# Layer 1's output, router and shared expert in blocks of 16 steps beside the recurrence

## The chip, the cores and the metric

The kernel runs on one core of a Trainium2 chip. The engines are PE (TensorE, matrix products; PEld is its weight load), DVE (VectorE), ACT (ScalarE), POOL (GpSimd) and SP (SyncE, which here only issues DMAs). The metric is the time of one execution in device microseconds; lower is better. The time before is the median of three runs.

## The reference, cut to what matters

The network has four layers on x (16 sequences of 128 steps, 256 features); each layer adds a mixing part and a feed-forward part to x. The change lies in layer 1. Its mixing part is a recurrence over the 128 steps, its feed-forward part a mixture of 64 experts, of which each token takes eight, and a shared expert:

```
def step(carry, xs):                      # 128 steps, all 16 sequences at once
    r, state = carry
    r = decay * r + kt * vt
    inp = (qt * r) @ Wi.T + bi
    gate = sigmoid(inp @ Wg.T + bg)
    blended = gate * state + (1 - gate) * inp
    state = tanh(blended @ A.T + inp @ Bm.T)
    out = state @ Wo.T + bo               # added to x

h = layernorm(x)                          # 2048 tokens of 256
logits = h @ router_w.T                   # 64 experts
topk_w, topk_ids = top_k(softmax(logits), 8)
topk_w = topk_w / sum(topk_w)
# each expert takes its first 128 tokens, in the order of the tokens
routed = segment_sum(expert(h[token]) * topk_w)
shared = silu(h @ ws_gate) * (h @ ws_up) @ ws_down
x = x + routed + shared
```

Only `gate * state`, the product with A and the tanh depend on the step before. Everything else of the recurrence is known ahead of it.

## The kernel before, in words

x stays in SBUF as 16 blocks of 128 rows by 256: block b is sequence b, a row is a step. A scheduler orders each engine's instructions from the order in which the program writes them and from what they depend on; it may pull an instruction ahead. `issue_after(i)` keeps what is written in it behind instruction i on i's engine.

**Layer 0** ends in `l0_rest`. It also makes, with `l1_pre`, what the recurrence needs of each step: `gate` and `pre`. Both have the layout (step, half of the features, sequence).

**The recurrence** is `l1_steps`. For each step PE adds `pre` (product with the identity) and `gate` times A (the products `ps_all<-wA,gate`) into a PSUM bank, one of three; ACT makes the tanh `th` (L964); DVE turns it into `state` (L966); DVE multiplies the next step's gate by it (L969); PE goes on with that. Beside it runs `side_work`: it makes ahead what layers 2 and 3 need of the context (keys, values, gates, head means, quantised weights). Its parts are closures with an engine, a cost and a gap, and `spread` gives each a step: a chain's parts follow each other, and the costs of one engine in one step stay under its `room`. In step s the parts are issued behind the last product, the tanh and the gate of that step.

**Behind the recurrence** come, for each sequence, the bias `bo` (L189, which nothing keeps behind the recurrence, so it stands where layer 0 ends), the output product of its 128 states with Wo, and the addition to x (L186). `l1_ffn` then takes four sequences at a time: norm (L161 to L170, the power on POOL at L152), a store of h to `rows` in DRAM, transpositions (L182), the router's products, the eight largest logits of each token (L1031) and the mask of the chosen (L1032, L1033). `l1_keys` turns the mask around, expert by token, and multiplies it by a falling count of the tokens (L1238). `l1_slots` takes the 128 largest keys of each expert in 16 rounds of MAX8 and 15 of MATCH_REPLACE (L1269, L1271) and turns them into `slot_tok`, a table of token numbers (L1287). Beside this run the weights of the chosen experts and the shared expert (`l1_widen`, `l1_narrow`), which is added to x; x is then stored to the first of three sums in DRAM.

**The experts**, `l1_experts`: for each of 32 pairs, POOL gathers the rows of both experts with `slot_tok` (L1102), PE transposes and multiplies, and POOL scatters the results with addition into the sums (L1159). Weights come over SP into a ring of 10 slots and 2 more (L1096 to L1100), four pairs ahead in the program. `l1_clear` fills the sums with zeros first (L1076). `l1_sum` loads x and the other two sums back (L1400, L1402) for layers 2 and 3, `l2_l3`.

Of the kernel before, what the change touches and what calls it, by code (L numbers as in the profile page):

```python
# [19 lines left out]
P = 128  # L20
# [10 lines left out]
RING, MORE = 10, 2  # L31
# [28 lines left out]
class Kernel:  # L60
    def __init__(self, ctx, tc, ins, out):
# [14 lines left out]
        self.wscale = self.pers.tile([P, 3], F32, name="wscale")  # L76
        self.ring = False

# [25 lines left out]
    def mm(self, out, lhsT, rhs, start=True, stop=True):  # L104
        return self.nc.tensor.matmul(out, lhsT, rhs, start=start, stop=stop)  # L105
# [49 lines left out]
    def norm_x(self, g):  # L155

        nc = self.nc
        st = self.small.tile([P, GB, 6], F32, tag="st", name="st")
        mv = self.small.tile([P, GB, 2], F32, tag="mv", name="mv")
        for i in range(GB):  # L160
            nc.vector.bn_stats(st[:, i], self.x[:, g * GB + i])  # L161
            nc.vector.bn_aggr(mv[:, i], st[:, i])
        r = self.rstd(mv[:, :, 1], GB)

        def end():
            less = self.small.tile([P, GB], F32, tag="less", name="less")
            nc.vector.scalar_tensor_tensor(less, mv[:, :, 0], -1.0, r, ALU.mult, ALU.mult)
            h = self.hpool.tile([P, GB, D], F32, tag="h", name="h")
            for i in range(GB):
                nc.scalar.activation(  # L170
                    h[:, i], self.x[:, g * GB + i], AF.Identity, bias=less[:, i:i + 1], scale=r[:, i:i + 1]
                )
            return h

        return end

    def transpose4(self, h, dst, g):

        for c in range(2):
            pt = self.psum("tp")  # L180
            for i in range(GB):
                self.nc.tensor.transpose(pt[:, i * P:(i + 1) * P], h[:, i, c * P:(c + 1) * P], self.ident)  # L182
            self.evac(dst[:, c, g * GT:(g + 1) * GT], pt)

# [10 lines left out]
    def front(self):  # L195
        right = self.right
        with ExitStack() as base:
# [12 lines left out]
            self.wpool = self.open(self.mids, "wring", RING)  # L210
            pool = self.open(right, "state", side="right")
            with ExitStack() as ctx:
                self.l1_steps(pool, rec, self.side_work(self.open(ctx, "side", 2)))
# [15 lines left out]
    def side_work(self, pool):  # L229
        nc, ins = self.nc, self.ins  # L230

        def load(**args):

            self.side_dma = nc.sync.dma_start(**args)

        self.pool = pool
        bank = {n: self.psum("mm") for n in ("turn", "keys", "gates", "ones")}
# [19 lines left out]
        def pair(p):  # L257
# [3 lines left out]
            def begin():  # L261
                s["c"] = self.ctx_pair(p)
                s["st"] = self.small.tile([P, 2, 6], F32, tag="st", name="st")
                s["mv"] = self.small.tile([P, 2, 2], F32, tag="mv", name="mv")
# [8 lines left out]

            def scale(i):
                if not i:
                    s["h"] = pool.tile([P, 2, D], F32, tag="h", name="h")
                nc.vector.tensor_scalar(
                    s["h"][:, i], s["c"][:, i], s["mv"][:, i, 0:1], s["r"][:, i:i + 1], ALU.subtract, ALU.mult
                )

            def turn():
                for c in range(2):
                    for i in range(2):
                        at = (c * 2 + i) * P
                        nc.tensor.transpose(bank["turn"][:, at:at + P], s["h"][:, i, c * P:(c + 1) * P], self.ident)

            def affine(c):
                if not c:
                    s["ct"] = pool.tile([P, 2, 2 * P], F32, tag="ct", name="ct")
                nc.scalar.activation(  # L290
                    s["ct"][:, c], bank["turn"][:, c * 2 * P:(c + 1) * 2 * P], AF.Identity,
# [3 lines left out]
            def keys(c):  # L295
                self.mm(bank["keys"][:, :2 * P], wk[:, c], s["ct"][:, c], c == 0, c == 1)

            def values():
                for bb in range(2):
                    at = 2 * P + bb * 64  # L300
                    for c in range(2):
                        self.mm(
                            bank["keys"][:, at:at + 64], s["ct"][:, c, bb * P:(bb + 1) * P], wv[:, c], c == 0, c == 1
                        )

            def keep():
                kvt = pool.tile([P, 3 * P], F32, tag="kvt", name="kvt")
                nc.scalar.copy(kvt, bank["keys"][:, :3 * P])
# [10 lines left out]
            def less():  # L319
                va = pool.tile([P, 2, 4, 65], F32, tag="va", name="va", bufs=2)  # L320
                nc.gpsimd.memset(va[:, :, :, 64:65], 1.0)
                nc.vector.tensor_tensor(
# [7 lines left out]
                ("DVE", 0.2, lambda: spread(0), 0), ("DVE", 0.4, lambda: spread(1), 2),  # L330
                ("DVE", 0.45, lambda: scale(0), 0), ("DVE", 0.45, lambda: scale(1), 0), ("PE", 0.45, turn, 0),
                ("ACT", 0.6, lambda: affine(0), 0), ("ACT", 0.6, lambda: affine(1), 0),
                ("PE", 0.43, lambda: keys(0), 0), ("PE", 0.43, lambda: keys(1), 0), ("PE", 0.45, values, 0),
                ("ACT", 0.5, keep, 0), ("DVE", 0.7, mean, 0), ("DVE", 0.2, share, 0), ("DVE", 0.7, less, 0),
            ]

        def group(g):
# [7 lines left out]
            def part(n, k):  # L345
                for b in range(GB):
                    self.mm(
                        bank["gates"][b * 32:b * 32 + 32, n * P:(n + 1) * P], wgate[:, k, n],
                        s["c"][:, k, b * P:(b + 1) * P], k == 0, k == 1,
                    )  # L350

            def keep():
                gc = pool.tile([P, 2 * P], F32, tag="gc", name="gc", bufs=1)
                nc.scalar.copy(gc, bank["gates"][:, :2 * P])
                load(out=self.gc_d[g], in_=gc)

            return [("SP", 0, begin, 3)] + [
                ("PE", 0.6, lambda n=n, k=k: part(n, k), 0) for n in range(2) for k in range(2)
            ] + [("ACT", 0.4, keep, 0)]

        def quantised(n, name):
# [5 lines left out]
            def begin():  # L367
                s["w"] = self.slot()[:, :2048]
# [7 lines left out]
            def total(i):  # L376
                nc.vector.tensor_reduce(
                    s["sums"][:, i:i + 1], quarter(i), AX.X, ALU.add, apply_absolute_value=True
                )

            def all_rows():
                for i in range(4):
                    self.mm(bank["ones"][:, :1], ones, s["sums"][:, i:i + 1], i == 0, i == 3)

            def scales():
                nc.vector.tensor_scalar(scale, bank["ones"][:, :1], 1.0 / (D * 1024), 1e-5, ALU.mult, ALU.max)
# [14 lines left out]
            return [("SP", 0, begin, 9)] + [("DVE", 0.65, lambda i=i: total(i), 0) for i in range(4)] + [  # L401
# [9 lines left out]
        for p in range(NB // 2):  # L411
            chains.append((1 + 13 * p, pair(p)))
            if p % 2:
                chains.append((13 * p - 5, group(p // 2)))
            if p % 2 == 0 and p < 6:
                chains.append((2 + 13 * p, quantised(p // 2, f"L2_ffn_w_{('gate', 'up', 'down')[p // 2]}T")))
        return self.spread(chains)

    def spread(self, chains):


        room = {"PE": 0.9, "ACT": 0.9, "DVE": 0.75, "SP": 1.0}
        used, out = {}, {}
        for at, parts in chains:
            last = None
            for engine, cost, f, gap in parts:
                if engine == "PE" and last in ("ACT", "DVE"):
                    at += 1
                last = engine
                while used.get((at, engine), 0.0) + cost > room[engine]:  # L430
                    at += 1
                used[at, engine] = used.get((at, engine), 0.0) + cost
                out.setdefault(at, []).append(f)
                at += 1 + gap
        return out
# [418 lines left out]


# [84 lines left out]
    def l1_steps(self, pool, rec, beside):  # L940
# [4 lines left out]
        wa, wo, gate, pre = w["A"], w["Wo"], w["gate"], w["pre"]  # L945
        state = pool.tile([P, 2, (P + 1) * NB], F32, name="state", bufs=1)
        sums = [self.psum("mm") for _ in range(3)]
        for ps in sums:
            nc.vector.memset(ps[:, :64], 0.0)
        for s in range(P):  # L950
            ps = sums[s % 3]
# [20 lines left out]
            if s in beside:  # L972

                with ExitStack() as order:
                    for i in (last, tanh, gated):
                        order.enter_context(self.tc.issue_after(i.ins))
                    for f in beside.pop(s):
                        f()
        for s in sorted(beside):
            for f in beside[s]:  # L980
                f()
        for b in range(NB):
            self.bias_to_x(b, w["bo"])

        def out(b):
            po = self.psum("mm")
            for c in range(2):
                self.mm(po[:, :D], state[:, c, b:P * NB:NB], wo[:, c], c == 0, c == 1)
            self.add_to_x(b, po[:, :D])

        self.l1_out = out


    def l1_ffn(self):
# [3 lines left out]
        nc, ins = self.nc, self.ins  # L998
        with self.tc.issue_after(self.side_dma.ins):
            rw, wsgu, wsd = self.weights(  # L1000
                "L1_ffn_router_wT", "L1_ffn_ws_gate_up", ins["L1_ffn_ws_down"].rearrange("(c p) n -> p c n", p=F1)
            )
        rows, sums = self.rows, self.expert_sums
        with self.tc.tile_pool(name="l1s", bufs=1, reuse_waits="tile") as keep:
            with self.tc.tile_pool(name="l1f", bufs=2, reuse_waits="tile") as pool:
                self.hpool = pool
                self.ht = pool.tile([P, 2, NTOK], F32, name="ht", bufs=1)
                lg = pool.tile([P, NB, NE], F32, name="lg", bufs=1)


                val = keep.tile([P, NB, TOPK], F32, name="val", bufs=1)
                pairs = pool.tile([P, NB // 2, 2, NE], F32, name="pairs", bufs=1)
# [1052 lines left out]
```

## Time and profile before

| | us |
|---|---|
| median of 3 runs (lowest, highest) | 1722.08 (1721.45, 1724.77) |
| the profiled execution | 1721.37 |
| its span | 1719.6 |
| layer 0, to 614 | 614 |
| recurrence, first tanh 614.14, last 800.25 | 187 |
| output, norm, router, 801 to 838.6 | 37.6 |
| search to first gather, 838.6 to 884 | 45.4 |
| experts, 884 to 1097 | 213 |
| layers 2 and 3, from 1097 | 623 |

The times of single instructions come from the profiled execution. A line of a timeline has the start and the duration in us, engine, line, operation, the tile that is written `<-` the tiles that are read, the shapes, a count, and in brackets how long the engine stood idle before it and what ended that. A line of a tile's view has the smallest, median and largest duration in ns and the starts of the first and the last. PEclk is the clock that was granted to PE, as a share of the full one.

### The profile page before, as it was taken

How to read it: one execution, taken by the hardware profiler on the slowest of the kernel's cores; microseconds unless marked ns; L12 is line 12 of the kernel's file. 1: busy time of each engine (PE TensorE's matmuls, PEld its weight loads, DVE VectorE, ACT ScalarE, POOL GpSimd, SP SyncE). 2: the span in 40 equal slices, each digit the busy share in tenths (PEclk: the TensorE clock that was granted, in tenths of full speed). 3: DMA queues.
4: the chain of work that ended last, by engine and by line, in shares of the span. 5: the costliest groups of instructions: out<-in, count | busy, mean ns of one | idle time of the engine just before them, and what ended most of it. 6: DMA issues, size and time to landing. Idle time of an engine off the chain costs nothing.

```text
span 1719.6 us, 29806 instructions
## 1 busy us (share of the span) xinstructions
PE 1540.7 (90%) x11567; PEld 1078.4 (63%) x11567; DVE 924.0 (54%) x2374; ACT 720.7 (42%) x2096; POOL 431.1 (25%) x423
## 2 busy tenths in 40 slices
PE   7999999998999887787889888348999999999998
PEld 5777776765444444445558666136777777777776
DVE  4565464557475545545852222267676665755641
ACT  1443343344343222222312222035556756766655
POOL 2001000002232300000447888411321321412211
PEclk9999999999999977867989999668999999999999
DMA  8000000100000211114699995860000100100000
GB/s 252 7 7 7 7 7 1 50 13 23 0 1 2 77 41 64 64 51 176 198 289 288 294 248 94 193 205 18 21 29 21 24 24 27 30 11 9 7 7 13
DMA packets 93053, 124.67 MB, mean 72 GB/s; under 512 B 19760, under 2 KB 73072, under 8 KB 92784
## 3 DMA queue, kind: packets, MB, share of 16 engines
q1 hardware_dynamic: 73072, 97.69, 17.9%
q0 software_dynamic: 12288, 18.88, 5.7%
q10 hardware_dynamic: 7552, 6.20, 1.1%
q8 instruction: 91, 1.49, 0.3%
q14 instruction: 50, 0.41, 0.1%
HBM read 94.68 MB, written 28.05 MB: 71 GB/s over the span
## 4 chain that ended last, share of the span: by engine, by line
PE 62%; DVE 15%; issue 8%; DMA 7%; POOL 4%; ACT 4%; SPq 0%; ACTq 0%; POOLq 0%; DVEq 0%
PE ps_all L105 40%; PE ps_mm L105 12%; DMA xg<-rows,slot_tok 3%; PE ps_av L105 2%; DMA sum<-y,slot_tok 2%; PE ps_sc L105 2%; POOL rstd L152 1%; DVE state L966 1%; PE ps_all L1818 1%; ACT th L964 1%; PE ps_tp L456 1%; DVE gate L969 1%; DMA w<-in_moe_down 1%; PE ps_all L1432 1%; DVE st L1410 1%
## 5 line engine op out<-in xcount | busy, mean ns | idle before, releaser
L152 POOL TENSOR_TENSOR rstd<-ve,nhalf 128x2 f32<-128x2 f32 (+2 forms) x77 | 58.0, 756 | 634.1 <-DVE ve L150 548.7
L1810 POOL TENSOR_TENSOR e<-e,rs 128x512 f32<-128x512 f32 x64 | 66.1, 1040 | 282.2 <-DVE rs L1809 266.5
L445 ACT ACTIVATE e<-ps_sc,nmax 128x128 f32<-128x128 f32 x256 | 89.9, 377 | 108.1 <-DVE nmax L441 108.1
L1159 POOL DMA_INDIRECT sum<-y,slot_tok x64 | 102.0, 1594 | 28.2 <-issue 13.1
L1807 ACT ACTIVATE e<-e,nmax 128x128 f32<-128x128 f32 x256 | 99.3, 391 | 11.7 <-DVE nmax L1798 11.3
L105 PE MATMUL ps_all<-xt,w 128*64 128x128 f32 (+1 forms) x1024 | 101.9, 286 | 1.6 <-issue 0.9
L105 PEld LDWEIGHTS ps_all<-xt,w 128*64 128x64 f32 (+1 forms) x1024 | 90.1, 169 | 16.4 <-issue 11.7
L964 ACT ACTIVATE th<-ps_all 128x64 f32<-128x64 f32 x128 | 28.6, 223 | 139.3 <-PE ps_all L105 138.2
L105 PE MATMUL ps_all<-wA,gate 128*16 128x64 f32 x2032 | 67.5, 268 | 14.4 <-DVE gate L969 9.1
L966 DVE STREAM_TRANSPOSE state<-th 128x64 f32<-128x64 f32 x128 | 31.4, 245 | 88.7 <-ACT th L964 88.7
L1432 PE MATMUL ps_all<-ident,h 128*128 128x128 f32 x168 | 29.1, 300 | 50.6 <-DVE h L1415 38.9
L105 PE MATMUL ps_all<-ident,pre 128*16 128x64 f32 x1024 | 46.8, 264 | 28.7 <-ACT th L964 27.6
L105 PE MATMUL ps_mm<-ht,wq 128*128 128x256 f32 x256 | 69.8, 396 | 0.7 <-ACT ht L113 0.7
L1102 POOL DMA_INDIRECT xg<-rows,slot_tok x64 | 63.6, 993 | 25.5 <-issue 9.7
L186 DVE TENSOR_TENSOR x<-x,ps_all 128x256 f32<-128x256 f32 x48 | 20.0, 416 | 93.0 <-PE ps_all L105 92.9
L105 PE MATMUL ps_mm<-ctxt,wk 128*128 128x256 f32 x256 | 66.8, 384 | 0.0
L105 PE MATMUL ps_mm<-wu,mt 128*128 128x256 f32 x256 | 66.0, 391 | 0.0
L105 PEld LDWEIGHTS ps_all<-wA,gate 128*16 128x16 f32 x2032 | 40.3, 115 | 38.7 <-DVE gate L969 38.3
L1415 DVE TENSOR_SCALAR h<-x,mv,rstd 128x256 f32<-128x256 f32 x112 | 46.2, 441 | 30.6 <-POOL rstd L152 29.9
L105 PE MATMUL ps_all<-ht,w3q 128*128 128x256 f32 x256 | 61.5, 389 | 0.7 <-ACT ht L1761 0.7
L1432 PEld LDWEIGHTS ps_all<-ident,h 128*128 128x128 f32 x168 | 19.8, 148 | 66.5 <-DVE h L1415 32.2
L105 PE MATMUL ps_all<-ht,w3v 128*128 128x256 f32 x256 | 60.9, 381 | 0.0
(364 smaller groups left out, 3706.4 us busy)
## 6 DMA issues: line engine op xcount, KB each, us to landing
w<-in_moe_gate_up SPq DMA_DIRECT2D x64, 384.0 KB
w<-in_moe_down SPq DMA_DIRECT2D x64, 96.0 KB
c_in<-in_ctx SPq DMA_DIRECT2D x16, 256.0 KB
sum<-w SPq DMA_DIRECT2D x8, 512.0 KB
w<-in_moe_down SPq DMA_DIRECT2D x64, 64.0 KB
ysum<-sum SPq DMA_DIRECT2D x16, 256.0 KB
low<-tops SPq DMA_DIRECT2D x12, 256.0 KB
va_d<-va SPq DMA_DIRECT2D x8, 260.0 KB
```

What stands on the lines that cost most here:

```text
L105: return self.nc.tensor.matmul(out, lhsT, rhs, start=start, stop=stop)
L152: nc.gpsimd.tensor_tensor(r, ve, self.nhalf[:, :n], ALU.pow)
L186: self.nc.vector.tensor_tensor(self.x[:, b], self.x[:, b], ps, ALU.add)
L445: nc.scalar.activation(e[:, i], src[:, i], AF.Exp, bias=nmax[:, i:i + 1], accum_out=ssum[:, i:i + 1])
L964: tanh = nc.scalar.activation(th, ps[:, :64], AF.Tanh)
L966: nc.vector.transpose(state[:, :, at:at + 32], th.rearrange("p (c n) -> p c n", c=2))
L1102: nc.gpsimd.indirect_dma_start(out=x, out_offset=None, in_=rows, in_offset=bass.IndirectOffsetOnAxis(ap=slot_tok[:, e:e + 1], axis=0),)
L1159: nc.gpsimd.indirect_dma_start(out=sums[e % len(sums)], out_offset=bass.IndirectOffsetOnAxis(ap=slot_tok[:, e:e + 1], axis=0), in_=y, in_o ...
L1415: nc.vector.tensor_scalar(h[:, i], src[:, i], mv[:, i, 0:1], r[:, i:i + 1], ALU.subtract, ALU.mult)
L1432: self.nc.tensor.transpose(pt[:, at:at + P], h[:, i, c * P:(c + 1) * P], self.ident)
L1807: nc.scalar.activation(e[:, i], e[:, i], AF.Exp, bias=nmax[:, i:i + 1], accum_out=ssum[:, i:i + 1])
L1810: nc.gpsimd.tensor_tensor(e, e, rs.unsqueeze(2).to_broadcast([P, 4, P]), ALU.mult)
```

## The change

x is turned to another order before the recurrence, so that a block of 128 rows is 16 steps of 8 sequences instead of 128 steps of one. Once 16 steps of the recurrence are done, everything of layer 1 that these 256 tokens need can be made: output product, bias, norm, router, best eight, keys, and for blocks 0 to 5 the shared expert. These are parts for `spread` like those of `side_work`. Block 7 and the shared expert of blocks 6 and 7 come behind the last step.

- `l0_rest`: x is stored to DRAM in the order (half of the sequences, step, sequence) and loaded back as 16 tiles of 128 tokens, on SP. Block q has the tiles q and q + 8.
- `l1_steps`: two PSUM banks for the sums instead of three, six for the beside work. Each block gives an urgent chain, from step 16q + 17, and a later one. PE's instructions in the parts keep the order in which they are written.
- `spread`: more room (ACT 1.15 for 0.9, DVE 0.95 for 0.75, POOL 1.4 is new), and stretches between "+T" and "-T" hold a PSUM bank alone.
- `side_work`: the scaling of h and the absolute sums of the weights go from DVE to ACT, the difference of the head means from DVE to POOL; the key products are one part; chains start every 10 steps instead of 13. The quantised weights use a buffer of the side pool instead of the ring.
- The silu of the shared expert is made of a tanh in the blocks.
- The ring of the expert weights is opened after the side pool is closed. Three slots that held the router's tables, logits and keys join it behind `l1_slots` (15 slots for 12).
- `l1_slots` turns token numbers into the new row order; `l1_sum` reads the sums in that order.

```diff
 # front
-            self.wpool = self.open(self.mids, "wring", RING)
+            self.keep = self.open(self.mids, "tables", OLD)
             pool = self.open(right, "state", side="right")
             with ExitStack() as ctx:
-                self.l1_steps(pool, rec, self.side_work(self.open(ctx, "side", 2)))
+                self.l1_steps(pool, rec, self.open(ctx, "side", 2))
+            self.wpool = self.open(self.mids, "wring", RING)
             with self.tc.issue_after(self.side_dma.ins):
                 self.l1_clear()
 # side_work
-                nc.vector.tensor_scalar(
-                    s["h"][:, i], s["c"][:, i], s["mv"][:, i, 0:1], s["r"][:, i:i + 1], ALU.subtract, ALU.mult
+                nc.scalar.activation(
+                    s["h"][:, i], s["c"][:, i], AF.Identity, bias=s["less"][:, i:i + 1], scale=s["r"][:, i:i + 1]
                 )
...
-                nc.vector.tensor_tensor(
+                nc.gpsimd.tensor_tensor(
                     va[:, :, :, :64].rearrange("p b h d -> p (b h) d"), s["heads"],
...
-                ("PE", 0.43, lambda: keys(0), 0), ("PE", 0.43, lambda: keys(1), 0), ("PE", 0.45, values, 0),
+                ("PE", 0.86, keys, 0, "+K"), ("PE", 0.45, values, 0), ("ACT", 0.5, keep, 0, "-K"),
+                ("DVE", 0.7, mean, 0), ("DVE", 0.2, share, 0), ("POOL", 1.4, less, 0),
...
-            return [("SP", 0, begin, 9)] + [("DVE", 0.65, lambda i=i: total(i), 0) for i in range(4)] + [
+            return [("SP", 0, begin, 9)] + [("ACT", 0.65, lambda i=i: total(i), 0) for i in range(4)] + [
                 ("PE", 0.4, all_rows, 0), ("DVE", 0.4, scales, 0)
 # spread
-        room = {"PE": 0.9, "ACT": 0.9, "DVE": 0.75, "SP": 1.0}
+        room = {"PE": 0.9, "ACT": 1.15, "DVE": 0.95, "POOL": 1.4, "SP": 1.0}
 # l0_rest
+        by_half = x_t.rearrange("(h s b) d -> h s b d", h=2, s=P)
+        for g in range(NG):
+            at = g % 2 * GB
+            nc.sync.dma_start(out=by_half[g // 2, :, at:at + GB], in_=self.x[:, g * GB:(g + 1) * GB])
+        by_tile = x_t.rearrange("(t p) d -> p t d", p=P)
+        for at in range(0, 8, 2):
+            for half in range(2):
+                ts = slice(half * 8 + at, half * 8 + at + 2)
+                nc.sync.dma_start(out=self.x[:, ts], in_=by_tile[:, ts])
 # l1_steps
-        sums = [self.psum("mm") for _ in range(3)]
+        sums = [self.psum("mm") for _ in range(2)]
+        self.bank = {n: self.psum("mm") for n in "KDEATC"}
+        blocks = [self.l1_block(side, q) for q in range(8)]
+        urgent = [(16 * q + 17, blocks[q][0]) for q in range(7)]
+        out, ends = self.spread(urgent)
+        shared = [(ends[q] - 6, blocks[q][1]) for q in range(6)]
+        beside, _ = self.spread(urgent + shared + self.side_work(side))
...
+        self.pinned = True
         for s in sorted(beside):
             for f in beside[s]:
                 f()
-        for b in range(NB):
-            self.bias_to_x(b, w["bo"])
+        for part in blocks[7][0]:
+            part[2]()
+        self.pinned = False
+    def l1_block(self, pool, q):
+        xs = self.x[:, q:q + 9:8]
+        def begin():
+            s["st"] = pool.tile([P, 2, 2, P], F32, tag="st", name="st")
+            for c in range(2):
+                src = self.state[:, c, q * 256:(q + 1) * 256].rearrange("p (s h b) -> p h s b", s=16, h=2)
+                for h in range(2):
+                    dst = s["st"][:, h, c].rearrange("p (s b) -> p s b", s=16)
+                    if q < 7:
+                        nc.gpsimd.tensor_copy(dst, src[:, h])
...
+        def bias():
+            nc.gpsimd.tensor_tensor(xs, xs, w["bo"].unsqueeze(1).to_broadcast([P, 2, D]), ALU.add)
+        def out(h):
+            for c in range(2):
+                self.mm(bank["A"][:, h * D:(h + 1) * D], s["st"][:, h, c], w["Wo"][:, c], c == 0, c == 1)
...
+        return [
+            ("POOL", 1.4, begin, 0), ("POOL", 1.3, bias, 0), ("PE", 0.86, lambda: out(0), 0, "+A"),
+            ("PE", 0.86, lambda: out(1), 0), ("DVE", 0.5, lambda: add(0), 0), ("DVE", 0.5, lambda: add(1), 0, "-A"),
+            ("DVE", 0.5, lambda: stats(0), 0), ("DVE", 0.5, lambda: stats(1), 0), ("DVE", 0.6, spread, 2),
+            ("DVE", 0.2, shift, 0), ("ACT", 0.55, lambda: norm(0), 0), ("ACT", 0.55, lambda: norm(1), 0),
+            ("PE", 0.45, turn, 0, "+T"), ("ACT", 0.65, even, 0, "-T"), ("PE", 0.45, router, 0), ("DVE", 0.65, best, 0),
+            ("DVE", 0.65, chosen, 0), ("PE", 0.2, turn_chosen, 0), ("DVE", 0.3, keys, 0),
+        ], [
+            ("PE", 0.86, lambda: widen(0, 0), 0, "+D"), ("PE", 0.86, lambda: widen(0, 1), 0),
+            ("PE", 0.86, lambda: widen(1, 0), 0), ("PE", 0.86, lambda: widen(1, 1), 0), ("ACT", 0.65, tanh, 0),
+            ("DVE", 0.75, silu, 0), ("DVE", 0.75, hidden, 0, "-D"), ("PE", 0.86, lambda: narrow(0), 0, "+A"),
+            ("PE", 0.86, lambda: narrow(1), 0), ("DVE", 0.75, end, 0, "-A"),
+        ]
 # l1_slots
-        nc.vector.tensor_copy(slot_tok, slot)
+        nc.vector.tensor_copy(tok, slot)
+        nc.vector.tensor_scalar(low, tok, P - 1, 3, ALU.bitwise_and, ALU.logical_shift_left)
+        nc.vector.tensor_scalar(mid, tok, 7, 7, ALU.logical_shift_right, ALU.bitwise_and)
+        nc.vector.tensor_scalar(tok, tok, 3072, None, ALU.bitwise_and)
+        nc.vector.tensor_tensor(low, low, mid, ALU.bitwise_or)
+        nc.vector.tensor_tensor(slot_tok, low, tok, ALU.bitwise_or)
```

In a block's chain `out`, `add`, `stats`, `spread`, `shift`, `norm`, `turn`, `even`, `router`, `best`, `chosen`, `turn_chosen` and `keys` do for its two tiles what `l1_ffn` and `l1_keys` did for four or for all; `spread` there is the statistics' end with the power on POOL. In the shared chain `widen` and `narrow` are the two layers, `tanh`, `silu` and `hidden` what lies between, and `end` adds to x and stores it.

## The prediction

> **What bounds the kernel now.** I read the page's chain, then the busy time by stretch, then the timeline of single steps, then who waits for whom in the expert stage. The stretches, cut at the last row before the recurrence, its end, the first search round (L1269), the first gather (L1102) and the last scatter's end (start:end, length, busy us of PE, PEld, DVE, ACT, POOL with counts, PE clock, DMA share, GB/s):
>
> ```profile
> 614.00:801.00 187.00, 143.91 (x3325) 82.42 (x3319) 96.07 (x378) 47.30 (x168) 6.15 (x14) 0.71 0.19 67
> 801.00:838.60 37.60, 31.41 (x171) 28.47 (x172) 26.96 (x127) 11.82 (x21) 9.21 (x14) 0.90 0.63 201
> 838.60:884.00 45.40, 40.35 (x120) 21.58 (x119) 41.50 (x55) 15.03 (x24) 22.65 (x18) 0.95 0.81 245
> 884.00:1097.00 213.00, 176.45 (x1420) 136.72 (x1418) 50.50 (x114) 45.65 (x112) 165.55 (x128) 0.94 0.89 227
> ```
>
> The recurrence is a latency loop, at a clock of 0.71 only; a step with the PE at full clock takes 1.27 us (tanh to tanh):
>
> ```profile
> 681.44 0.22 ACT L964 ACTIVATE th<-ps_all 128x64 f32<-128x64 f32 x1 [0.59 <-PE ps_all L105]
> 681.69 0.24 DVE L966 STREAM_TRANSPOSE state<-th 128x64 f32<-128x64 f32 x1 [0.71 <-ACT th L964]
> 681.97 0.19 DVE L969 TENSOR_TENSOR gate<-gate,state 128x32 f32<-128x32 f32 x1
> 682.22 0.42 PE L105 MATMUL ps_all<-wA,gate 128*16 128x64 f32 x16 [0.20 <-DVE gate L969]
> ```
>
> At half clock (tanh at 624.32 and 625.80) it is 1.48, with 1.54 where the side work is heavier. From 801 the output products, norm and router run alone for 37.6 us; 41 us of DVE search follow, and this is what slot_tok and the first gather wait for. The expert stage then runs at the pace of POOL, which has two gathers and two scatters for each pair of experts, 6.4 us a pair, with 0.30 between them:
>
> ```profile
> 917.08 1.62 POOL L1159 DMA_INDIRECT sum<-y,slot_tok  x1 [0.30 <-issue]
> 919.00 1.57 POOL L1159 DMA_INDIRECT sum<-y,slot_tok  x1 [0.30 <-DMA sum<-y,slot_tok]
> 920.88 1.02 POOL L1102 DMA_INDIRECT xg<-rows,slot_tok  x1 [0.30 <-PE ps_all L105]
> 922.20 0.98 POOL L1102 DMA_INDIRECT xg<-rows,slot_tok  x1 [0.30 <-PE ps_all L1112]
> ```
>
> DMA is as full (0.89), but weights are issued ahead to 1022 and used to 1082. So everything from the gather on moves as slot_tok moves.
>
> **1. End of layer 0.** The additions of bo (L189) leave. They stand on the chain at 586.01 and hold POOL, so the next rstd starts at 588.29 though its input was ready before 587:
>
> ```profile
> 586.01 2.31 POOL L189 TENSOR_TENSOR x<-x,bc_bo 128x256 f32<-128x256 f32 x2 [0.53 <-DVE h L1415]
> 588.29 0.70 POOL L152 TENSOR_TENSOR rstd<-ve,nhalf 128x2 f32<-128x2 f32 x1
> ```
>
> Gain 2 us (0 to 2.3). The turn of x through DRAM (2 MB out, 2 MB back, SP queue) can start when x is last read, about 590. At the 252 GB/s of the page's first slice it takes 17 us; DMA is idle from 580 to 600, and block 0 wants x at step 18, about 640. Hidden. Queued behind it on SP are the side loads; wgate's addition on DVE waits for one, and cost step 3 a 1.74 once. If it is late the recurrence waits: 0 to 8 us, I take 0.
>
> **2. The recurrence.** spread is arithmetic, so I filled the new plan with its own costs. Before step 128 it holds 56 steps with a PE part of 0.86 (two products of 256 columns; out, widen, narrow, keys), 10 with a router or values part alone, 2 with all_rows, 5 with such a part and a turn, 55 lighter. The plan's costs aren't durations. Eight passes of 128 weights by 64 columns (values; a router part is the same) are 1.04 from the first to the next pre product, and one product of 256 columns is 0.63:
>
> ```profile
> 642.72 0.70 PE L105 MATMUL ps_all<-ct,wk 128*128 128x256 f32 x2
> 643.35 0.31 PE L105 MATMUL ps_all<-ident,pre 128*16 128x64 f32 x8
> 645.25 1.10 PE L105 MATMUL ps_all<-wv,ct 128*128 128x64 f32 x8
> 646.29 0.30 PE L105 MATMUL ps_all<-ident,pre 128*16 128x64 f32 x8
> ```
>
> A PE-bound step is 0.35 (start of the wA products to the side part) + the part + 0.12 (pre to the next wA). Values: 1.51, and the trace has 1.49. The 0.86 part, which no step shows alone, lies between 0.86 (bare passes) and 1.06 (0.63 and two passes of 0.215 more): step 1.33 to 1.53; I take 1.48, nearer the row with its changeover. With a turn: 2.0.
> 56x1.48 + 5x2.0 + 12x1.5 + 55x1.27 = 82.9 + 10 + 18 + 69.9 = 180.8. About 20 light steps (2 to 15, 27 to 32) stay at half clock: 20x0.21 = 4. In 14 steps ACT gets 1.12 to 1.15 beside its tanh of 0.22, more than 1.27: 2. Sum 187, against 186.1 (614.14 to 800.25).
>
> The clock decides whether 1.48 is right. At half clock the x2 product takes 1.15 (756.76 to 757.91), so an 0.86 step is about 2.75. With the clock mix of the row above, 58% at half, 56x0.58x1.27 = 41 us come on top: 1750. The Trainium skill (TensorE: Matmul & The Clock Gate, Part 1) says that the gate opens after some 3.4 us of busy PE. I take the rule: steps 107 to 110 are PE-full at half clock (1.92, 1.92, 2.68, 2.13) and step 111 is back at 1.26.
>
> A rule speaks against the change. SBUF — State Buffer, "Who interferes with whom": a DVE instruction with two SBUF inputs and a GpSimd instruction that reads SBUF exclude each other for the whole instruction. L969, in the loop, has two SBUF inputs. Today its row shows no such loss, but POOL does only 6 us of work there:
>
> ```profile
> L969 DVE TENSOR_TENSOR gate<-gate,state x127: 182/192/194, 614.7 to 799.3; 128x32 f32<-128x32 f32 x127
> ```
>
> Elsewhere the trace does show it; this addition of 0.17 ends when POOL's product ends:
>
> ```profile
> 1138.76 1.27 POOL L1627 TENSOR_TENSOR sq<-sq,bc_lnw 128x512 f32<-128x512 f32 x1 [0.86 <-DMA wlow<-in_L_ffn_U]
> 1138.94 1.11 DVE L1611 TENSOR_TENSOR n<-n 128x8 f32<-128x8 f32 x1
> ```
>
> The change puts into the loop 7 bias additions and 8 va differences of 128x512 (1.27 each), 28 copies of some 0.28 (0.73 for 128x512, L734, with a quarter the size) and 15 powers of 0.7. By L969's row the cost is 0. By the rule: a va difference follows share, 0.4 after a gate, and reaches 0.3 past the next one (8x0.3); a bias addition follows the four copies, about where the next gate falls, and holds it 0 to 1.2, say 0.6 (7x0.6). 6.6, with 7 powers that reach 0.1 over 7 us. Taken: 7. Recurrence 194, +8 (0 to +27).
>
> **3. The tail.** After step 127 the plan has the end of block 5's shared expert and block 6 from norm to keys; then block 7 whole. PE keeps the written order, so block 7's out waits for block 6's last transposition. Hop by hop, with rows of L182, L1026, L1031, L1032, L170 and those above: narrow 1.8, turn 0.55, copy 0.65, router 1.1, best 0.7, chosen 0.9, transposition 0.25: 6. Then out 1.8, add 0.5, statistics 0.9, power 0.8, shift 0.25, two norms 1.1, turn to keys 4.9: 10.2. 16 at full clock, 18 with half clock in places (12 to 22; 12 if block 7 need not wait). It replaces 800.7 to 838.6: -20.
>
> **4. The search** stays at its rounds, which wait only for each other:
>
> ```profile
> L1269 DVE MAX8 top<-key x16: 1185/1228/1229, 838.6 to 878.9; 128x8 f32<-128x1024 f32 x16
> L1271 DVE MATCH_REPLACE8 key<-top,key x15: 1207/1208/1210, 840.0 to 877.7; 128x1024 f32<-128x1024 f32 x15
> ```
>
> Turning tokens to the new rows adds 5 DVE instructions of 0.2 (row of the CAST, L1287): +1. Gate weights and blocks 6 and 7 of the shared expert lie beside it as before.
>
> **5. Expert weights.** Their ring is now opened on the side pool's space, so the zeros and weights start at about the end of the tail, some 25 us later against the recurrence's end than today's. In the 47 us to the first gather 290 GB/s bring 13.6 MB, of which 4.4 are zeros: 8 pairs ahead instead of 11. Later 29.5 MB per 100 us (rows 900 to 1000) less gathers and scatters bring 17 pairs while POOL takes 15.6. Cost 0. The three ring slots more and two y buffers fewer: POOL sets the pace, 0. Behind the experts nothing changes.
>
> **Sum**: -2 + 8 - 20 + 1 = -13, on the profiled execution's 1721.4: 1708. The median shown is 0.7 higher: **1709**.
>
> **Rivals.** *A (0.5)*, as summed, 1700 to 1718. *B (0.2)*, the beside work is nearly free: 0.86 steps at 1.35 (-7), no port loss (-7): 1695. For it: DVE and ACT have room; against: steps with values already stretch. *C (0.2)*, slower: POOL holds the gate. If 15 operations of 1.27 each cost 1.1 and 15 powers 0.5 (16.5 + 7.5, and copies 2), 26 instead of 7: 1728. It decides from 20 us of port loss on, or 0.7 a POOL operation. For it: L1611. Against: POOL starts are tied to the step, as today's powers, which always miss the gate. *D (0.1)*, the experts start earlier but end as before, because their weights are late: 1721. Against: rates in 5; today's weights end 60 us early.
>
> The range goes from B to C: 1694 to 1730; A's own is 1700 to 1718. 0.2% is 3.4 us, about what a measurement tells from no change. Faster: A and B, less A's edge, 0.69; same: D and edges, 0.1; slower: 0.21.
>
> **What would show it.** Recurrence 194 long, steps of 1.48 with 0.86 parts, clock 0.9 or more; L969's longest rows near 1 us beside POOL; first MAX8 18 us after the last tanh; gathers to last scatter still 211. A recurrence over 210 with a low clock or many long L969 rows makes me wrong; so does a first gather that waits for rows or weights.

## The result, and the profile after

The changed kernel takes 1713.12 us (median of 5 runs, 1709.21 to 1714.96) against 1722.08 (1719.65 to 1724.77): 0.9946 of the time before, 95% interval 0.9928 to 0.9963. That is 9 us less; 1709 was forecast. The profiled execution took 1709.21, the fastest of the five, with a span of 1707.4, 12.2 less than the span before.

The busy time by stretch of the changed kernel, cut at the first and last tanh, the first search round (L1386), the first gather and the start of the last scatter (columns as before):

```profile
612.00:803.00 191.00, 172.09 (x3728) 116.17 (x3729) 110.11 (x479) 74.62 (x235) 27.44 (x56) 0.90 0.18 62
803.00:827.00 24.00, 17.39 (x48) 11.42 (x47) 6.72 (x39) 5.12 (x11) 5.39 (x9) 0.51 0.38 109
827.00:872.80 45.80, 9.78 (x30) 5.03 (x28) 42.18 (x59) 6.30 (x8) 9.36 (x8) 0.64 0.90 280
872.80:1084.00 211.20, 172.79 (x1408) 134.27 (x1408) 49.08 (x112) 45.75 (x112) 165.68 (x128) 0.94 0.94 242
```

The granted clock in the recurrence went from 0.71 to 0.90, and the stretch of 24 us behind it has the lowest clock of the four, 0.51. Where the 12.2 us between the two profiled executions are (forecast: what the prediction gave for the stretch):

| | before | after | difference | forecast |
|---|---|---|---|---|
| first tanh at | 614.1 | 612.4 | -1.7 | -2 |
| first to last tanh | 186.1 | 189.9 | +3.8 | +8 |
| last tanh to first MAX8 | 38.4 | 24.6 | -13.8 | -20 |
| first MAX8 to first gather | 45.4 | 45.9 | +0.5 | +1 |
| first gather to last scatter | 211.4 | 208.4 | -2.9 | 0 |
| from there to the end of the span | 624.2 | 626.2 | +2 | 0 |

**The recurrence.** Step n lasts from its tanh to the next one; a light step has little or no PE work beside the recurrence, a heavy one a part of 0.86. Steps at full clock are about as long as the forecast took them. But steps 2 to 12 and most of 16 to 31 run at half clock. The timeline of the changed kernel where two heavy steps, 19 and 20, fall into that stretch:

```profile
640.05 0.22 ACT L995 ACTIVATE th<-ps_all 128x64 f32<-128x64 f32 x1 [0.85 <-PE ps_all L107]
...
641.83 0.65 PE L107 MATMUL ps_all<-wA,gate 128*16 128x64 f32 x16
642.42 2.08 PE L107 MATMUL ps_all<-wWo,st 128*128 128x256 f32 x4
642.55 0.22 ACT L995 ACTIVATE th<-ps_all 128x64 f32<-128x64 f32 x1 [1.83 <-PE ps_all L107]
...
644.98 1.34 PE L107 MATMUL ps_all<-wWo,st 128*128 128x256 f32 x4
645.12 0.22 ACT L995 ACTIVATE th<-ps_all 128x64 f32<-128x64 f32 x1 [2.34 <-PE ps_all L107]
```

From tanh to tanh it is 2.50 and 2.57. The output product of block 0 takes 2.08 the first time and 1.34 the second, when the clock is coming back.

**The gate and POOL.** One line's instructions each: the gate, the va differences and the bias additions, with their shortest, median and longest ns and the first and last start:

```profile
L1000 DVE TENSOR_TENSOR gate<-gate,state x127: 191/192/194, 613.0 to 801.6; 128x32 f32<-128x32 f32 x127
L300 POOL TENSOR_TENSOR va<-c_in,mean x8: 1042/1044/1208, 657.1 to 791.0; 128x512 f32<-128x512 f32 x8
L1076 POOL TENSOR_TENSOR x<-x,bc_bo x8: 1265/1269/1486, 590.3 to 603.1; 128x512 f32<-128x512 f32 x8
```

No gate is longer than 194 ns. The bias additions stand at 590 to 603, ahead of the recurrence: nothing in the code ties them to an instruction of a step on their own engine, POOL, and the scheduler put them early.

**The tail.** The timeline of PE, from the last recurrence products, with the one DVE operation that block 7's last transposition waits for:

```profile
801.81 0.42 PE L107 MATMUL ps_all<-wA,gate 128*16 128x64 f32 x16 [0.85 <-DVE gate L1000]
802.41 3.76 PE L107 MATMUL ps_all<-wsd,act 96*128 96x256 f32 x8 [0.18 <-DVE act L1166]
805.97 1.06 PE L111 MATMUL ps_all<-ident,h 128*128 128x128 f32 x4
807.70 1.97 PE L107 MATMUL ps_all<-w 128*128 128x64 f32 x8 [0.67 <-ACT w L1120]
811.16 0.48 PE L111 MATMUL ps_all<-ident,w 128*128 128x128 f32 x1 [1.49 <-DVE w L1139]
811.43 3.62 PE L107 MATMUL ps_all<-wWo,st 128*128 128x256 f32 x8
818.80 1.39 PE L111 MATMUL ps_all<-ident,h 128*128 128x128 f32 x4 [3.75 <-ACT h L1103]
820.87 5.44 PE L107 MATMUL ps_all<-w 128*128 128x64 f32 x12 [0.68 <-ACT w L1120]
823.98 0.29 DVE L1139 TENSOR_TENSOR w<-w 128x128 f32<-128x128 f32 x1
826.10 0.40 PE L111 MATMUL ps_all<-ident,w 128*128 128x128 f32 x1
```

Block 7's output product (811.43) has its operand at 803.9 and waits for block 6's last transposition (811.16). A router takes 1.97 instead of the 1.10 of full clock, block 5's last shared product 3.76 instead of 1.89 (both from e_best2 below). The row at 820.87 is block 7's router with the first shared products of blocks 6 and 7, which stand between it and block 7's last transposition: the mask for it is ready at 824.27, and it starts at 826.10.

### The profile page after: what moved, and what is told of

Its sections match the earlier page's. It is cut to its first block, busy times and chain, and to the rows that moved or that the text cites. A ratio compares the mean times of both kernels' runs of the same rounds, so it can differ in the third digit from the quotient of the medians.

```text
span 1707.4 us, 30266 instructions
## 1 busy us (share of the span) xinstructions
PE 1519.3 (89%) x11743; PEld 1076.5 (63%) x11743; DVE 916.0 (54%) x2390; ACT 733.3 (43%) x2133; POOL 436.3 (26%) x445
## 5 line engine op out<-in xcount | busy, mean ns | idle before, releaser
L159 POOL TENSOR_TENSOR rstd<-ve,nhalf 128x2 f32<-128x2 f32 (+1 forms) x81 | 60.3, 748 | 628.5 <-DVE ve L157 525.0
L1932 ACT ACTIVATE e<-e,nmax 128x128 f32<-128x128 f32 x256 | 99.3, 391 | 12.0 <-DVE nmax L1923 11.5
L107 PE MATMUL ps_all<-wA,gate 128*16 128x64 f32 x2032 | 58.4, 235 | 7.6 <-DVE gate L1000 5.9
L163 DVE TENSOR_TENSOR x<-x,ps_all 128x256 f32<-128x256 f32 x32 | 13.4, 418 | 89.3 <-PE ps_all L107 89.3
L107 PE MATMUL ps_all<-ht,w3g 128*128 128x256 f32 x256 | 60.5, 379 | 0.0
L1945 ACT COPY et<-ps_all 128x512 f32<-128x512 f32 x64 | 35.3, 587 | 55.3 <-PE ps_all L1943 55.2
L107 PE MATMUL ps_all<-w3n,act 128*128 128x256 f32 x256 | 58.5, 381 | 0.0
```

Source lines behind the costliest of these rows:

```text
L107: i = self.nc.tensor.matmul(out, lhsT, rhs, start=start, stop=stop)
L159: nc.gpsimd.tensor_tensor(r, ve, self.nhalf[:, :n], ALU.pow)
L1932: nc.scalar.activation(e[:, i], e[:, i], AF.Exp, bias=nmax[:, i:i + 1], accum_out=ssum[:, i:i + 1])
L1945: nc.scalar.copy(et[par], pt)
```

## The experiments

The other runs were taken later, in four groups (a_again, e_tail, e_noshared, e_warm; e_best, e_noshared_warm, e_ring12, e_bias; e_before_warm, b_again, e_best2; e_best3). The kernel before ran in each group too, with medians of 1720 to 1731 us, so what is compared is the ratio to it within the group, with its 95% interval in brackets, and stretches of the traces. "Recurrence" is first to last tanh, "tail" is last tanh to first MAX8, "stage" is first gather to last scatter.

**The changed kernel again** (a_again).

> The changed kernel unchanged, so that the runs below stand beside it on one chip. Theory: recurrence 190 us (first to last tanh), tail 24 from the end of the states to the first MAX8, median 1709 to 1716. No theory expects otherwise.

1720.9 us, ratio 0.9945 (0.9923 to 0.9968), as at first. Recurrence 193.5, 3.7 longer: in this execution steps 96 to 99 also fell to half clock and took 2.56, 2.78, 2.78 and 2.41. Tail 24.4. The recurrence's row:

```profile
612.00:806.00 194.00, 174.42 (x3727) 117.35 (x3727) 109.80 (x476) 74.08 (x233) 27.17 (x56) 0.89 0.18 61
```

**The tail's written order** (e_tail). `n6` and `n7` are the parts of blocks 6 and 7 that come behind the last step, `s5` is the rest of block 5's shared expert.

```
- for s in sorted(beside): for f in beside[s]: f()
- for part in blocks[7][0]: part[2]()
+ for f in (n7[:4] + n6[:3] + n7[4:9] + n6[3:5] + n7[9:12]
+           + n6[5:7] + n7[12:14] + n6[7:] + n7[14:] + s5): f()
...
+ with self.tc.issue_after(self.turned.ins):
      self.l1_shared(hidden)
```

> Block 7's output products are written ahead of block 6's last parts, the two blocks' hops alternate on PE, block 5's last shared products go behind both, and so do the shared expert's products of blocks 6 and 7. Theory 'written order': the tail is 24 us because block 7 waits 7.5 us for PE's order and 1.8 us for the shared products, so it falls to 15 to 18 and the median by 6 to 9. Rival 'half clock': each hop is long because PE idles and the gate is shut, the same hops stay in a row, so the tail stays 21 to 24 and the median within 3 of the changed kernel.

Tail 16.0, time 1711.98, ratio 0.989 (0.9867 to 0.9913): 9 us under a_again. The stretch behind the recurrence, 806 to 822, shows that the clock did not cause this:

```profile
806.00:822.00 16.00, 10.17 (x42) 7.74 (x37) 6.34 (x40) 5.14 (x10) 3.29 (x8) 0.61 0.33 90
```

It is still 0.61 (0.59 in a_again). At this half clock the written order cost 8.4 us of tail; 1.0 of it comes back in the search, which takes 46.9 to the first gather instead of 45.9.

**Less work in the loop** (e_noshared): `widen`, `tanh`, `silu`, `hidden` and `narrow` return at once, `end` only stores. The kernel leaves the shared expert of blocks 0 to 5 out.

> The shared expert of blocks 0 to 5 is left out of the loop (its PE products, tanh, silu and additions), the rest of the plan stands where it stood. Theory 'a part of 0.86 stretches its step from 1.27 to 1.5': 36 steps get lighter by 0.23, but at full clock, so the recurrence falls by 6 to 9, to 181 to 184. Rival 'PE beside work keeps the clock up': with 36 steps lighter the clock falls back to half and a light step takes 1.48, so the recurrence stays at 188 to 192, with a mean clock below 0.85.

The recurrence became longer: 198.4 against 193.5 in a_again, time 1725.8 against 1720.9, ratio 0.9963 (0.9942 to 0.9983). The rival named the clock, and even it expected no loss. The recurrence's row:

```profile
613.00:812.00 199.00, 162.04 (x3591) 106.62 (x3590) 99.78 (x460) 71.87 (x228) 27.40 (x56) 0.78 0.18 61
```

136 PE instructions fewer than in a_again's row, and the clock at 0.78 instead of 0.89: it falls in more places, and heavy steps that remain there take 2.5 to 3.3.

**Work that nobody reads** (e_warm).

```
+ if s in (1, ..., 9, 14, ..., 19, 23, ..., 29, 32):
+     with self.tc.issue_after(last.ins):
+         for k in range(2):
+             for j in range(4):
+                 nc.tensor.matmul(bank["E"][32j:32j+32, :64],
+                     w["Wo"][:, k, 32j:32j+32], w["Wo"][:, 1, :64])
```

> In 23 light steps among 1 to 32, 8 products of 32 by 64 columns whose result nobody reads go behind the recurrence's own on PE. Theory 'the first 34 steps run at half clock because PE has too little to do': the clock of steps 2 to 32 rises from 0.6 to over 0.85, heavy steps 19 and 20 fall from 2.5 to 1.5 and the light ones from 1.48 to 1.3, so the recurrence falls by 4 to 7. Rival 'the clock of the first steps is the throttle's choice after layer 0, or the filler costs what it saves': recurrence within 2 of 190, clock below 0.75 there.

1708.68, ratio 0.9869 (0.9848 to 0.9889), recurrence 185.4, 8 less than in a_again; the tail is 2.8 shorter too, which this edit does not explain. The first 40 us:

```profile
612.00:652.00 40.00, 32.14 (x1164) 21.96 (x1164) 19.58 (x89) 14.90 (x51) 4.25 (x8) 1.00 0.08 25
```

The clock is 1.00 there (0.66 in the changed kernel): 1164 PE instructions in these 40 us instead of 712, and steps 2 to 12 take 1.27 instead of 1.48, the two heavy ones 1.61 and 1.41 instead of 2.50 and 2.57. Steps 96 to 98, which have no filler near them, still take 2.58, 2.78 and 2.12.

**Both together, and less work at full clock** (e_best, e_noshared_warm). The filler now goes into unused columns of the recurrence's own PSUM banks.

> The tail's order of e_tail and the filler products, now in all 46 steps whose plan has less than 0.5 of PE work. Theory 'the shut gate and the written order are two separate losses': they add, recurrence 180 to 183 us (also the 4 us of steps 98 to 101 go), tail 15 or less, and the time is 17 to 22 below the changed kernel's, so about 0.980 of the kernel before. Rival 'one cause': the tail's gain was already the clock's, so together they give no more than the larger one, 0.987.

1701.85, ratio 0.982 (0.9796 to 0.9845); tail 13.8, recurrence 184.8. The gains add, and go below the 0.987 of the rival, so they are two losses. Recurrence and ratio fall a little short of what was expected (180 to 183, 0.980): filler beside parts of 0.4 and more stretched 13 steps to 1.71 to 1.79.

> The shared expert of blocks 0 to 5 left out, as in e_noshared, with the filler products in the 80 steps that have less than 0.5 of PE work then. Theory 'e_noshared gained nothing because the gate shut': at full clock the light parts pay, and the recurrence falls from 198 to 172 to 178, clock 0.97 or more. Rival 'the steps are bound by something else than PE': 190 or more at a high clock.

One execution only, so its trace is read and not its time:

```profile
613.00:791.00 178.00, 140.32 (x4870) 105.50 (x4870) 99.63 (x459) 71.36 (x228) 27.32 (x56) 1.00 0.21 69
```

Recurrence 177.5 at a clock of 1.00, 7.3 below e_best: with the clock held, the same omission that cost 5 us gains 7.

**The filler in the kernel before** (e_before_warm, b_again).

> The kernel before, with the filler products in the 79 steps of its recurrence that have no PE work in its plan; nothing of the change. Theory 'the recurrence before ran at half clock because PE had too little to do': clock 0.95 or more, recurrence 168 to 172 instead of 186, time 14 to 20 below the kernel before (ratio 0.988 to 0.992), as much as the whole change brought. Rival 'the clock rose in the changed kernel for another reason': recurrence 182 or more.

> The kernel before, unchanged, for a trace from this chip. Theory 'the expert stage is POOL's pace and the 3 us by which it was shorter are the spread between chips and runs': first gather to last scatter 213 to 218, like the kernels with the change on this chip. Rival 'the change shortens it': 217 to 221, 3 above them.

1704.99, ratio 0.9885 (0.9843 to 0.9926). The recurrence's rows, first of the kernel before in the same group (b_again), then with filler:

```profile
614.00:801.00 187.00, 143.93 (x3314) 82.53 (x3312) 95.83 (x377) 47.03 (x167) 6.17 (x14) 0.70 0.19 65
```

```profile
615.00:782.00 167.00, 121.64 (x4557) 85.09 (x4561) 95.75 (x377) 46.88 (x167) 6.15 (x14) 0.99 0.21 69
```

From 187.3 to 167.6. By the medians this gives some 20 us without anything of the change, where the whole change gives 9; the intervals of the two ratios just touch. It also tells what the change's beside work costs at full clock: 182.2 (e_best2 below) less 167.6, 14.6 us, of which the changed kernel shows only 4 to 6, because that work also raises the clock.

Expert stage: 211.4 in b_again, below the 213 to 218 that was expected, and 209.3 to 217.6 in the kernels with the change. The 2.9 us by which it was shorter at first lie inside that spread; that the change shortens it is not shown.

**The ring of 12** (e_ring12): `at = ep % (RING + MORE)`.

> The expert weights use 12 slots again, not the 15 of the change. Theory 'POOL sets the pace of the expert stage': first gather to last scatter within 1.5 us of the other kernels of this batch, time within 2 of the changed kernel. Rival 'the longer ring is where the stage's 3 us came from': the stage is 3 us longer.

Stage 214.5, between e_bias (213.3) and e_best (217.3) of the same group, so not 3 us longer than with the longer ring; the 1.5 us that were expected between kernels do not hold either, e_best is 2.9 away. Time 1716.95, ratio 0.9902 (0.9873 to 0.9932); this interval overlaps with that of a_again, so no loss is seen, and a gain is not shown.

**The additions of bo inside the loop** (e_bias; the edit is shortened).

```
+ s["copied"] = nc.gpsimd.tensor_copy(dst, src[:, h])
...
+ with self.tc.issue_after(s["copied"].ins):
      nc.gpsimd.tensor_tensor(xs, xs, bo, ALU.add)
```

> The additions of bo (POOL, 128x512) of blocks 0 to 6 are tied behind the block's copies, so they run inside the recurrence instead of ahead of it. Theory 'POOL and the gate exclude each other on SBUF', as the prediction took it: gate rows of up to 1.2 us, 7 steps longer by 0.6 on the mean, recurrence +3 to +6. Rival 'the gate wins and POOL waits': gate rows stay below 0.2 us, some additions take longer than 1.27, recurrence within 1.5.

The timeline around block 3's addition:

```profile
710.34 0.25 DVE L997 STREAM_TRANSPOSE state<-th 128x64 f32<-128x64 f32 x1 [0.35 <-ACT th L995]
710.58 1.26 POOL L1083 TENSOR_TENSOR x<-x,bc_bo 128x512 f32<-128x512 f32 x1
710.62 1.27 DVE L1000 TENSOR_TENSOR gate<-gate,state 128x32 f32<-128x32 f32 x1
711.94 0.24 PEld L107 LDWEIGHTS ps_all<-wA,gate 128*16 128x16 f32 x16 [1.33 <-DVE gate L1000]
```

POOL begins 0.04 before the gate, and the gate of 0.19 takes 1.27; PE waits behind it, and the step takes 2.40 instead of 1.41. Six of the seven additions hit a gate (1.00 to 1.27), 5.6 us in all over the usual 0.19; beside a_again these six steps are 0.06 to 0.99 longer, 4.0 us in all. So the port theory holds and its rival falls. The recurrence is 196.1 against 194.9 (e_ring12) and 193.5 (a_again), but which steps lose the clock differs between these, and the time (ratio 0.9945, 0.9925 to 0.9966) doesn't show it; the gate rows do.

**Filler in the tail, and a stuck scalar** (e_best2, e_best3).

> As e_best, but the filler stands only in the 28 steps that have no PE work in the plan, and nine groups of it fill PE's waits in the tail. Theory: the steps that took 1.72 in e_best fall to 1.5 to 1.6 (about 10 of them: recurrence 182 to 184), and the tail's turn and router of block 7 fall from 1.39 and 1.96 to 0.6 and 1.04, so the tail is 11.5 to 13: time 2 to 4 below e_best, ratio 0.979 to 0.981. Rival 'fewer fillers let the gate shut again': some of steps 96 to 102 at 2.5 or more, recurrence over 186.

1693.21, ratio 0.981 (0.9777 to 0.9843), which can't be told from e_best's. Recurrence 182.2, at most 1.95 a step, so the rival falls:

```profile
614.00:797.00 183.00, 163.44 (x4174) 115.61 (x4174) 110.02 (x477) 74.23 (x233) 27.32 (x56) 0.99 0.20 65
```

The tail has a clock of 1.00 but takes 14.1, not 11.5 to 13. Its last hops:

```profile
807.97 1.93 POOL L1386 TENSOR_TENSOR w<-w 128x1024 f32<-128x1024 f32 x1 [5.03 <-DVE half L1790]
807.99 1.93 DVE L1791 TENSOR_TENSOR half<-half,wscale 128x1 f32<-128x1 f32 x1
...
809.99 0.22 DVE L1168 TENSOR_TENSOR w<-ps_all,w 128x128 f32<-128x128 f32 x1
810.66 1.23 DVE L1409 MAX8 top<-w 128x8 f32<-128x1024 f32 x1 [0.38 <-DVE const L1616]
```

A product of one column, for a scale of layer 2, takes 1.93 beside POOL's product and holds block 7's keys (L1168) behind it. In e_best the same product stood elsewhere, at 803.47, with no POOL work beside it, and took 0.15.

```
- nc.vector.tensor_tensor(half[:, 1:2], half[:, 0:1], wscale[:, 1:2], ALU.mult)
- nc.vector.tensor_scalar(half[:, 1:2], half[:, 1:2], 1.0 / 127.0, None, ALU.mult)
+ nc.vector.tensor_scalar(half[:, 1:2], half[:, 0:1], wscale[:, 1:2],
+                         1.0 / 127.0, ALU.mult, ALU.mult)
```

> As e_best2, with one edit at the tail's end: a DVE product of two SBUF tiles of one column (a scale that layer 2 needs later), which took 1.93 us beside POOL's 128x1024 product and held block 7's keys, is written with its second factor as the per-partition scalar of a one-input operation. Same place in DVE's order. Theory 'two SBUF tensor inputs are what POOL shuts out': it takes under 0.25 us beside the same POOL product, the keys come 1.7 us earlier, tail (last tanh to first MAX8) 12.0 to 12.8 instead of 14.2, ratio about 0.979 to 0.981. Rival 'any DVE operation that reads SBUF twice is shut out' or 'it waited for its data': it still takes 1.5 to 2, tail 14.

```profile
807.98 1.93 POOL L1386 TENSOR_TENSOR w<-w 128x1024 f32<-128x1024 f32 x1 [5.38 <-DVE half L1790]
808.00 0.21 DVE L1791 TENSOR_SCALAR half<-half,wscale 128x1 f32<-128x1 f32 x1
...
808.46 0.29 DVE L1168 TENSOR_TENSOR w<-ps_all,w 128x128 f32<-128x128 f32 x1
...
808.86 1.23 DVE L1409 MAX8 top<-w 128x8 f32<-128x1024 f32 x1
```

0.21 at the same place beside the same product; tail 12.7. The time is 1691.68, ratio 0.9828 (0.98 to 0.9855): from e_best2 it can't be told apart, and 1.7 us is a third of the half-width of such an interval. In the trace the search is 0.7 longer, because an addition to x now falls into its first round, and the recurrence is 183.7: step 20 fell to half clock in this execution and took 2.59, so the filler does not hold the clock every time. Either kernel is 1.7 to 1.9% below the kernel before, and over 1% below the changed one.

## Why the prediction was right, and where not

The sign, the size and the likeliest case held: 1713 and -9 us for 1709 and -13. Not all its terms did. The errors were of both signs, and that they nearly cancelled was luck.

**1, the end of layer 0:** -1.7 for -2. The additions of bo did not leave layer 0, but they now wait for the turned x, until 590, and the last rstd no longer waits for them. The turned x and the side loads were not late.

**2, the recurrence:** 189.9 and, in a_again, 193.5; 194 was forecast, but out of other terms. *The steps at full clock* were right: 0.86 parts 1.49 to 1.53 (1.48), a turn with values 1.87 to 1.94 (2.0), and the sum of 180.8 + 2 for a plan at full clock is near what e_best2 measures, 182.2. *The half clock* was too small: 4 us for some 20 light steps at 0.21. It counted no heavy step there, though the plan has parts of 0.4 to 0.86 from step 19 to 23 and the prediction itself gave 2.75 for such a step. Measured against e_best2 it is 7.6 us in the first trace and 11.3 in a_again, where the clock gate shut a second time near step 95. *The port* was 7 and is 0. The mechanism was right, as e_bias shows, and so was the price of the additions: 4.0 us of step time for the seven, where 0.6 each, 4.2, was forecast. The place was wrong. The prediction put the additions into the loop because the plan names a step for them, but an instruction is held there only if something ties it behind that step's instructions on its own engine, and POOL had no such tie. The va differences, reckoned at 0.3 each, end about when the gate starts (668.27 + 1.04 = 669.31; gate at 669.25). Two errors of about 4 and 7 cancelled in part, by luck.

**The clock rule.** The Trainium skill (TensorE: Matmul & The Clock Gate, Part 1) has the gate open after some 3.4 us of busy PE and shut after an idle window. The prediction used it to open the gate only, and its own row for it, steps 107 to 110, shows more than 3.4: the profile has PE busy without a gap from 768.0 to 777.2 there, 9.2 us at a granted clock of 0.50. In a_again it is 9.7 us (from 754.75), around step 19 of the changed kernel some 6, at step 20 of e_best3 only 3.2; so a step that meets the shut gate can pay for longer than the rule says. And no long idle stretch is needed to shut it. In a light step PE works 0.73 of 1.27 us (0.31 and 0.42) and stands idle for at most 0.4 at a time, and the traces show that this doesn't keep it open: steps 2 to 12 are shut in the changed kernel, and open in e_warm once 0.41 of filler is added. How much work is enough is not shown; in e_best2 steps 2 to 4 are shut in spite of filler.

**3, the tail:** -20 forecast, -13.8 measured; 18 us became 24.6. Two terms were too small. Half clock was charged 2 us, "in places", and was everywhere (0.51). Against the same work at full clock in e_best2 (1.89, 0.60, 1.10 and 1.99 for shared product, turn, router and output product), the rows at 802.41, 805.97, 807.70, 811.43 and 818.80 and block 7's router are 6.5 us longer in all. And the shared products of blocks 6 and 7, ready as soon as block 7's norm is turned, were not seen to slip in front of its last transposition: 1.8 us. The wait of block 7 for block 6, which e_tail removes, was in the forecast. The remark that the tail would be "12 if block 7 need not wait" was about right: 12.7 in e_best3, which has the order, the clock and the scalar's edit.

**4 and 5:** +0.5 for +1 (the slot operations cost 0.95 more, the rest was 0.5 shorter). With DMA at 0.94 PE waited for weights six times, by at most 1.7 us, and behind the first gathers POOL kept its pace, with at most 0.7 between operations; so weights did not set the stage, as said. That it took 2.9 us less, and what follows it 2.0 more, was not forecast, and the runs explain neither.

**Rivals.** B's first half (lighter steps) fell, its second (no port loss) came true. C had a mechanism that exists, but its price was too high (1.1 an operation; the seven additions of e_bias cost 0.8 each in gate rows and 0.6 in steps), and so was its extent: no gate is longer beside the va differences and the powers, so even with the additions in the loop it is 4 to 6 us, not 26. D fell with the first gather 11.2 us earlier and the end 12.2 earlier.

## What to carry to other kernels

In a latency loop read the granted clock before pricing work beside it: here steps with idle PE cost more than filled ones, so taking work out made the loop slower, and filler in the light steps alone brought the kernel before 1.15%. Then look at what follows the loop: with an engine that keeps the written order, two independent chains want their hops written alternately. And a plan that names a step moves nothing by itself: look in the timeline at which instructions are tied to it, above all POOL operations beside a two-input DVE operation on the critical path.

## What the hardware showed unexpectedly

- Leaving 36 steps' products out of the loop lengthened it by 5 us (clock 0.89 to 0.78); with filler the same omission shortened it by 7.
- Size does not matter for who is shut out: a DVE product of one column waited 1.93 us for POOL's product of 1024, since both its inputs are SBUF tensors, and took 0.21 when the second was a per-partition scalar. The Trainium skill (SBUF — State Buffer, "Who interferes with whom") says that the first to start keeps the port for its whole instruction; the rows agree, with POOL ahead by 0.02 and 0.04 us. In the changed kernel single POOL operations were the longer ones (a copy of L1069 up to 488 ns for a median of 293); what held them is not shown.
- The expert stage of kernels alike in it took 208.4 to 217.6 us from one execution to the next. What sets this stays open.
